# The first block of a graph-convolution kernel: its features loaded and cast in two halves, its slabs moved to the heads of two queues

## The chip, the cores and the metric

The kernel runs on one core of a Trainium2 chip. The metric is the device time of one execution in microseconds (us). The engines are named as in the profile: PE (TensorE matmul), PEld (its weight load), DVE (VectorE), ACT (ScalarE), POOL (GpSimd) and SP (SyncE, which here only issues loads).

## The reference, cut to what matters

Eight graphs share one sparse 2048 x 2048 adjacency matrix, whose nonzero values are equal within a row. Each of two layers multiplies the features by the matrix repeatedly, mixes the results with weights, adds the input and normalizes.

```
x: (8, 2048, 64)   adj: (2048, 2048), rows divided by their number of entries
# layer 0
A2  = 2 * (adj @ adj) - I
x_g = [x, adj x, A2 x]                        # per node
out = einsum('bnki,nkio->bno', x_g, w) + b    # w, b from the node's embedding
x   = layernorm(x + out)
# layer 1: five terms x, A x, (2 A A - I) x, and the last two again
x   = layernorm(x + concat(terms) @ weight + bias)
```

## The kernel before, in words

The nodes are cut into 16 tiles of 128. The adjacency matrix lies transposed in memory, so a slab `adj[h, k]` holds the 128 source nodes of tile k against one half h of the target nodes. A slab is not used as numbers: DVE turns it into zeros and ones (`places`, `tensor_scalar ... not_equal` with 0, written as float32r, into a tile `s`), and the row's common value, kept in `rcol`, is multiplied in when a sum leaves PSUM. The features of a tile (`z[0][k]`, 128 x 512) are split into a high part, a cast to float32r on ACT (`high`, line 250), and the remainder, a subtraction on DVE (`low`, line 254). Both parts are called `hl` and are the moving operand of the products.

The part of the kernel that matters here is the first hop, `hop_x(g, kk, j)`. It is run for g = 0, 1 (which quarter columns of the slabs are taken), kk = 0 to 7 and j = 0, 1, with k = kk + 8 j. So the first block works on tile 0 and the second on tile 8. One block is 16 products of 128 x 512: eight column groups i of the slab, each against the high and the low part (`add_block`, line 264). In the very first block the eight products with the high part come first, then the eight with the low part; from the second block on, the order is i by i, high then low. Group i = 0 to 3 of a g = 0 block reads `s[:, 0]` and i = 4 to 7 reads `s[:, 1]`.

`run` issues these steps in a hand-written order: the part `features` of a block four blocks ahead, `operands` two blocks ahead, `use` (the products) in its turn. Instructions wrapped in `ordered` or `load` stay in program order on their engine, so what is written later on DVE, ACT or SP waits for what is written earlier. In the first two blocks `features` loads two half slabs of 256 KB, `raws[0]` and `raws[1]`, each into its own one of the six `raw` buffers; later blocks load one tile of 512 KB.

Before all of this, `first_constants` loads the features of tile 0 (256 KB) and `rcol` (8 KB, 64 bytes for each partition) on the queue of ACT, while SP loads the slabs. It also loads ACT's function table and issues ten products on a tile of zeros (`WARM = 10`, line 145) so that TensorE is running before the first real product.

In the first block DVE runs `places` of the first half slab, then `low`, then `places` of the second half slab. In the second block it runs `low` and then both `places`:

```
high(z[0][k], hl)
if j == 1:
    low(z[0][k], hl)
for h in range(2):
    ordered(nc.vector.tensor_scalar(s[:, h], got["raws"][h], 0.0, None, ALU.not_equal))
    if h == 0 and j == 0:
        low(z[0][k], hl)
```

After the first hop come a second hop built on seven half-size products, the mixing of layer 0, and the same for layer 1 with a last stage that stores the output.

Of the kernel before, what the change touches and what calls it, by code (L numbers as in the profile page):

```python
# [9 lines left out]
F32 = mybir.dt.float32  # L10
# [4 lines left out]
ALU = mybir.AluOpType  # L15
# [3 lines left out]
P = 128  # L19
B, N, C = 8, 2048, 64  # L20
# [5 lines left out]
FIRST = 8  # L26
HL = 7
RAW = 6
WARM = 10
SLOTS = 3  # L30
SPLIT = 4096.0
SWAPPED = (0, 2, 1, 3, 4, 6, 5, 7)
# [9 lines left out]
def pattern(  # L42
# [22 lines left out]
    nc = tc.nc  # L65

    def pool(stack, name, bufs, **kw):
        return stack.enter_context(tc.tile_pool(name=name, bufs=bufs, **kw))
# [4 lines left out]
    rawp = pool(ctx, "fraw", RAW)  # L73
# [12 lines left out]
    def bank(name):  # L86

        return psum.tile([P, 2, 512], F32, tag="ps", name=name)
# [7 lines left out]
    z = [z0, [z1[:, t, :] for t in range(NT)], [z2[:, t, :] for t in range(NT)]]  # L96

    def bc(s, t):
        return z[s][t].rearrange("p (b c) -> p b c", c=C)


    rcol = keep.tile([P, NT], F32, tag="rcol", name="rcol")
# [21 lines left out]
    def load(q, to, src):  # L124
        return tc.keep_in_program_order(q.dma_start(out=to, in_=src))
# [3 lines left out]
    def ordered(ins):  # L129
        if in_order:  # L130
            tc.keep_in_program_order(ins)


    def first_constants():
        load(nc.scalar, z[0][0], x[0].rearrange("n b c -> n (b c)"))
        load(nc.scalar, rcol, rcols)
        nc.vector.memset(eps, EPS)

        tc.keep_in_program_order(nc.scalar.activation(root, eps, AF.Sqrt))

        idle = spool.tile([P, 5 * P], BF16, tag="s", name="idle")
        nc.vector.memset(idle, 0.0)
        first = bank("first")
        for _ in range(WARM):
            nc.tensor.matmul(first[:, 0, :], lhsT=idle[:, :P], rhs=idle[:, P:], start=True, stop=True)
        nc.vector.memset(part, 1.0 / C)
        nc.vector.memset(ident, 0.0)
        make_identity(nc, ident, nomemset=True)

    def node_bias(pb):  # L150

        eT, b0_sb = bias_sb, wl[:, 5]
        for j in range(4):
            for g in range(4):
                q = slice(32 * g, 32 * g + D)
                nc.tensor.matmul(  # L156
                    pb[g // 2][:, g % 2, j * C : (j + 1) * C], lhsT=eT[q, j * P : (j + 1) * P], rhs=b0_sb[q],
                    start=True, stop=True, tile_position=(32 * g, 0),
                )
# [67 lines left out]
    def load_slab(src, shape):  # L227
        raw = rawp.tile(shape, F32, tag="raw", name="raw")
        load(nc.sync, raw, src)
        return raw  # L230
# [6 lines left out]
    def places(raw):  # L237
        s = spool.tile(list(raw.shape), F32R, tag="s", name="s")
        ordered(nc.vector.tensor_scalar(s, raw, 0.0, None, ALU.not_equal))
        return s  # L240
# [8 lines left out]
    def high(src, to):  # L249
        ordered(nc.scalar.copy(to[0], src))  # L250

    def low(src, to):

        ordered(nc.vector.tensor_tensor(to[1], src, to[0], ALU.subtract))  # L254

    def halves(src, to=None):

        if to is None:
            to = [hpool.tile([P, B * C], F32R, tag="hl", name="hl") for _ in range(2)]
        high(src, to)  # L260
        low(src, to)
        return to

    def add_block(accs, s, hl, first, last):

        order = [(i, h) for i in range(len(accs)) for h in range(2)]
        if first:
            order.sort(key=lambda ih: ih[1])
        for i, h in order:
            nc.tensor.matmul(  # L270
                accs[i], lhsT=s[:, i * P : (i + 1) * P], rhs=hl[h],
                start=(first and h == 0), stop=(last and h == 1),
            )
# [19 lines left out]
    def banks(n):  # L293
        pairs = [bank("acc") for _ in range(n // 2)]
        return [p[:, i] for p in pairs for i in range(2)]
# [222 lines left out]
    Q = N // 4  # L518
    BC = B * C // 2
    KK = NT // 2  # L520
    first_constants()


    sums_of = scratch.tile([KK, 2, P, 4, Q], BF16, tag="sums", name="sums_of")
# [6 lines left out]
    def put_together(g, kk, x0, x1):  # L531
        to = z2[:, 2 * (kk % 8) : 2 * (kk % 8) + 2, :].rearrange("p t n -> p (t n)").bitcast(BF16)
        to = to.rearrange("p (i n) -> p i n", i=4)
        for i, (a, b, op) in enumerate((
            (x0[:, 1], x1[:, 1], ALU.add), (to[:, S1], x0[:, 0], ALU.subtract),
            (x1[:, 0], to[:, S2], ALU.subtract), (x0[:, 0], x0[:, 1], ALU.subtract),
        )):
            ordered(nc.vector.tensor_tensor(to[:, i], a, b, op))

        stores.append(lambda: ordered(nc.scalar.dma_start(out=sums_of[kk, g], in_=to)))  # L540

        for _ in range(2):
            if len(stores) > (1 if g else 6):
                stores.pop(0)()

    def hop_x(g, kk, j):
        k = kk + KK * j

        def features(got):
            if g == 0 and kk == 0:  # L550
                if j == 1:
                    load(nc.sync, z[0][k], x[k].rearrange("n b c -> n (b c)"))
                got["raws"] = [load_slab(adj[h, k, :, :Q], [P, Q]) for h in range(2)]

        def operands(got):
            if g == 0 and kk == 0:

                s = got["s"] = spool.tile([P, 2, Q], F32R, tag="s", name="s")
                hl = got["hl"] = [hpool.tile([P, B * C], F32R, tag="hl", name="hl") for _ in range(2)]
                high(z[0][k], hl)  # L560
                if j == 1:
                    low(z[0][k], hl)
                for h in range(2):
                    ordered(nc.vector.tensor_scalar(s[:, h], got["raws"][h], 0.0, None, ALU.not_equal))
                    if h == 0 and j == 0:
                        low(z[0][k], hl)
            else:
                if g == 0:
                    load(nc.sync, z[0][k], x[k].rearrange("n b c -> n (b c)"))
                raw = load_slab(adj[:, k, :, g * Q : (g + 1) * Q].rearrange("h m n -> m h n"), [P, 2, Q])  # L570
                got["s"] = places(raw)
                got["hl"] = halves(z[0][k])
                if g == 1 and len(loads) > 3:
                    load(nc.sync, *loads.pop(0))
            while due:
                due.pop(0)()
            couple.append(got["s"])
            if j == 1:
                due.append(lambda both=couple[:]: put_together(g, kk, *both))
                couple.clear()  # L580
                if g == 1 and kk == KK - 1:
                    due.pop(0)()

        def out(i):
            t = 4 * g + i if i < 4 else 4 * g + i + 4
            a, r = accs[i], rcol[:, t : t + 1]
            if i % 2 if g == 0 or i > 3 else i > 1:
                ordered(nc.vector.tensor_scalar_mul(z[1][t], a, r))
            else:
                ordered(nc.scalar.activation(z[1][t], a, AF.Copy, scale=r))  # L590

        def use(got):
            s, hl = got["s"], got["hl"]
            if kk == 0 and j == 0:
                accs[:] = banks(8)
            last = kk == KK - 1 and j == 1
            add_block(accs, s.rearrange("p h n -> p (h n)"), hl, kk == 0 and j == 0, last)
            if last:
                for i in range(8 if g == 0 else 4):
                    out(i)  # L600
            seen = xcpool.tile([P, 2, Q], BF16, tag="ln_xc", name="seen")
            i = g * NT + k
            ordered(nc.scalar.activation(seen, s, AF.Copy, accum_out=nonzero[:, i : i + 1]))
            if j == 1:
                ordered(nc.scalar.dma_start(out=quarters[kk, :, :, g, :], in_=seen))
            else:
                ordered(nc.scalar.dma_start(out=corner[kk, :, g, :], in_=seen[:, 0]))
            if k in centred and g == 1:
                centre_features(k)
            if last and g == 1:  # L610
                stores.pop(0)()

                todo.extend(lambda i=i: out(i) for i in range(4, 8))

        return [(4, features), (2, operands), (0, use)]


# [284 lines left out]
    s = ("load_sum", "operands")  # L902
    h, norm = None, None
# [3 lines left out]
    for t in range(NT):  # L907
        got, last = {}, t == NT - 1
# [62 lines left out]
        norm, h = norm_now, z[0][t]  # L971
# [487 lines left out]
```

## Time and profile before

| | |
|---|---|
| median of 4 runs | 751.27 us (750.83, 750.84, 751.69, 751.72) |
| the profiled execution | 750.95 us, of which the span from the first to the last instruction is 748.6 us |
| granted TensorE clock, mean | 0.997 |
| PE busy | 740.4 us, 99% of the span |
| DVE, ACT, POOL busy | 80%, 61%, 39% |
| first warming product, first real product | 1.29 us, 5.13 us |
| products of the first hop, lines L270 and `acc` | 512 in 116.61 us |

A share of busy time is an average over the whole span. What the first few microseconds contain is read from the timeline and from windows of half a microsecond. In the timeline, the columns are the start, the length, the engine, the line, the operation with what it writes and reads, the shape, the number of instructions that were merged into the line, and in brackets how long the engine had been idle and what ended that.

### The profile page before, as it was taken

The page shows a single profiled execution, that of the slowest core. Times are in us where ns is not written, and L with a number is a line of the kernel's source. Part 1 is how long each engine was busy: PE and PEld are TensorE (multiplying, and loading weights), DVE is VectorE, ACT ScalarE, POOL GpSimd, SP SyncE. Part 2 cuts the span into 40 slices and gives each one's busy share as a digit, 9 for nine tenths or more (in the row PEclk, how much of TensorE's full clock was granted, in tenths as well). Part 3 has the DMA queues.
Part 4 walks back from the last instruction along what each step waited for, and adds up shares of the span by engine and source line. Part 5 has one row for each costly group of instructions (what it writes and reads, how often), then busy time and mean ns, then how long its engine had stood idle before and what let it go on. Part 6 is the DMA issues. An engine that isn't in the chain of part 4 may idle for free.

```text
span 748.6 us, 13524 instructions
## 1 busy us (share of the span) xinstructions
PE 740.4 (99%) x4940; PEld 613.3 (82%) x4940; DVE 598.7 (80%) x954; ACT 456.7 (61%) x1123; POOL 293.2 (39%) x312
## 2 busy tenths in 40 slices
PE   9999999999999999999999999999999999999996
PEld 6888888888888888888888888888888888888885
DVE  6868888999978898888888888869588557778663
ACT  5445453878766677777777777778877662112111
POOL 0001110133233888888888888874000000021431
PEclk9999999999999999999999999999999999999998
DMA  8996997545420000000000000003444354665621
GB/s 313 354 381 214 377 385 258 179 158 165 159 86 15 17 15 16 18 17 26 6 25 15 16 15 1 2 29 128 136 159 146 136 168 142 176 184 176 197 99 46
DMA packets 73544, 96.47 MB, mean 129 GB/s; under 512 B 4864, under 2 KB 48384, under 8 KB 73344
## 3 DMA queue, kind: packets, MB, share of 16 engines
q1 hardware_dynamic: 62064, 76.66, 31.6%
q10 hardware_dynamic: 11408, 18.89, 6.8%
q8 instruction: 41, 0.67, 0.4%
q14 instruction: 31, 0.25, 0.1%
HBM read 76.65 MB, written 18.87 MB: 128 GB/s over the span
## 4 chain that ended last, share of the span: by engine, by line
PE 98%; DMA 0%; DVE 0%; ACT 0%; issue 0%; DVEq 0%; ACTq 0%
PE pm L426 35%; PE accT L707 27%; PE acc L270 16%; PE a L270 10%; PE accT L270 6%; PE pu L501 3%; PE pt L316 1%; PE accT L863 1%; DMA z<-in_x 0%; PE accT L501 0%; PE accT L156 0%; PE accT L316 0%; ACT hl L250 0%; DVE z L305 0%; DVE sq L1078 0%
## 5 line engine op out<-in xcount | busy, mean ns | idle before, releaser
L707 PE MATMUL accT<-s,hl 128*128 128x512 f32 x896 | 205.8, 391 | 0.0
L707 PEld LDWEIGHTS accT<-s,hl 128*128 128x128 f32 x896 | 167.5, 188 | 35.5 <-issue 0.5
L460 ACT ACTIVATE aside<-pm,pack_sb 128x128 f32<-128x128 f32 x512 | 141.8, 436 | 18.9 <-PE pm L426 16.3
L426 PE MATMUL pm<-wh,hl 64*128 64x512 f32 x768 | 151.6, 392 | 0.0
L426 PE MATMUL pm<-wm,parts 64*128 64x512 f32 x768 | 149.8, 387 | 0.0
L426 PE MATMUL pm<-wl,parts 64*128 64x512 f32 x768 | 149.6, 386 | 0.0
L694 ACT CAST s<-raw 128x1024 fp32r<-128x1024 bf16 x104 | 110.1, 1058 | 36.8 <-ACT hl L250 27.9
L270 PE MATMUL acc<-hl,s 128*128 128x512 f32 x512 | 116.6, 390 | 0.2 <-ACT hl L250 0.2
L476 DVE TENSOR_REDUCE sums<-aside 128x128 f32<-128x1024 f32 x96 | 112.6, 1213 | 1.4
L270 PEld LDWEIGHTS acc<-hl,s 128*128 128x128 f32 x512 | 95.9, 188 | 21.0 <-ACT hl L250 0.7
L447 DVE TENSOR_TENSOR aside<-pm,pack_sb 128x1024 f32<-128x1024 f32 x64 | 78.0, 1222 | 18.5 <-PE pm L426 18.1
L426 PEld LDWEIGHTS pm<-wm,parts 64*128 64x128 f32 x768 | 72.0, 184 | 15.3
L426 PEld LDWEIGHTS pm<-wh,hl 64*128 64x128 f32 x768 | 72.2, 185 | 14.7 <-issue 0.4
L426 PEld LDWEIGHTS pm<-wl,parts 64*128 64x128 f32 x768 | 72.1, 184 | 14.4
L250 ACT CAST hl<-z 128x256 fp32r<-128x256 f32 (+1 forms) x96 | 47.8, 516 | 58.4 <-PE acc L270 24.2
L406 POOL TENSOR_TENSOR s<-s,part 128x8 f32<-128x8 f32 x16 | 7.0, 440 | 172.8 <-DVE s L405 102.7
L270 PE MATMUL a<-hl,s 128*128 128x512 f32 (+1 forms) x352 | 73.4, 370 | 0.0
L254 DVE TENSOR_TENSOR hl<-z,hl 128x512 fp32r<-128x512 f32 (+1 forms) x96 | 58.0, 611 | 18.2 <-ACT hl L250 8.0
L465 POOL TENSOR_TENSOR aside<-aside 128x1024 f32<-128x1024 f32 (+2 forms) x48 | 70.9, 1477 | 2.5
L270 PEld LDWEIGHTS a<-hl,s 128*128 128x128 f32 x352 | 61.9, 188 | 11.3
L303 POOL TENSOR_TENSOR z<-z,got 128x512 f32<-128x512 f32 x3 | 4.8, 1624 | 143.4 <-ACT got L302 143.4
L371 ACT ACTIVATE sq<-z 128x512 f32<-128x512 f32 x31 | 20.0, 652 | 48.2 <-DVE z L305 46.9
(139 smaller groups left out, 955.2 us busy)
## 6 DMA issues: line engine op xcount, KB each, us to landing
raw<-in_adj SPq DMA_DIRECT2D x58, 512.0 KB, 6.0
raw<-sums_of SPq DMA_DIRECT2D x64, 256.0 KB, 2.7
sums_of<-z ACTq DMA_DIRECT2D x16, 512.0 KB, 7.4
raw<-quarters SPq DMA_DIRECT2D x32, 256.0 KB, 2.6
raw<-in_adj SPq DMA_DIRECT2D x16, 384.0 KB, 3.5
quarters<-seen ACTq DMA_DIRECT2D x16, 256.0 KB, 6.6
xt<-in_xT SPq DMA_DIRECT2D x16, 256.0 KB, 2.7
z<-in_x SPq DMA_DIRECT2D x15, 256.0 KB, 6.1
```

The costliest lines, as they stand in the source:

```text
L250: ordered(nc.scalar.copy(to[0], src))
L254: ordered(nc.vector.tensor_tensor(to[1], src, to[0], ALU.subtract))
L270: nc.tensor.matmul(accs[i], lhsT=s[:, i * P : (i + 1) * P], rhs=hl[h], start=(first and h == 0), stop=(last and h == 1),)
L371: ordered(nc.scalar.activation(sq, src, AF.Square))
L426: nc.tensor.matmul(pm[:, j], lhsT=tt[k][n][q, u, :], rhs=w_parts[n][k][q, ds, :], start=(k == 0 and n == 0), stop=(k == 2 and n == 2),)
L447: ordered(nc.vector.tensor_tensor(side_by_side(a), got, e, ALU.mult))
L460: ordered(nc.scalar.activation(to[d], got, AF.Copy, scale=emb_sb[:, t, h * DD + d : h * DD + d + 1]))
L465: ordered(nc.gpsimd.tensor_tensor(to, to, more, ALU.add))
L476: ordered(nc.vector.tensor_reduce(to, src, AX.X, ALU.add))
L501: nc.tensor.matmul(pm[:, j, i * 3 * C : (i + 1) * 3 * C], lhsT=hT[q, 2 * g + i, :], rhs=v[q], start=True, stop=True,)
L694: ordered(nc.scalar.copy(s, got["raw"]))
L707: nc.tensor.matmul(acc[i][:, c], lhsT=hl[h][:, i * P : (i + 1) * P], rhs=S[:, c * 512 : (c + 1) * 512], start=(kk == 0 and h == 0), stop=( ...
```

## The change

The features of tile 0 are loaded in two halves of 128 KB (the graphs 0 to 3 and 4 to 7): the first at the head of ACT's queue, the second on SP's queue behind the first half slab. The second half slab goes from SP's queue to ACT's, behind the first half of the features. The cast of tile 0 is divided: ACT casts the first half, DVE (`tensor_copy`) the second. `places` of the first half slab is cut into 128 and 384 columns, and the order on DVE in the first block becomes copy, `places` of 128, of 384 and of 512 columns, then `low`. The second block loads its slab as one transfer of 512 KB instead of two of 256 KB, and its order on DVE becomes `places`, `places`, `low`. `rcol` is loaded on SP's queue with the third pair of blocks. Seven warming products are issued instead of ten.

```diff
-WARM = 10
+WARM = 7
...
     def first_constants():
-        load(nc.scalar, z[0][0], x[0].rearrange("n b c -> n (b c)"))
-        load(nc.scalar, rcol, rcols)
+        raws = [rawp.tile([P, N // 4], F32, tag="raw", name="raw") for _ in range(2)]
+        halves_of_x = slice(0, B // 2), slice(B // 2, B)
+        load(nc.sync, raws[0], adj[0, 0, :, : N // 4])
+        for q, b in zip((nc.scalar, nc.sync), halves_of_x):
+            load(q, bc(0, 0)[:, b], x[0][:, b])
+        load(nc.scalar, raws[1], adj[1, 0, :, : N // 4])
...
+        return raws
...
-    first_constants()
+    first_raws = first_constants()
...
                 if j == 1:
                     load(nc.sync, z[0][k], x[k].rearrange("n b c -> n (b c)"))
-                got["raws"] = [load_slab(adj[h, k, :, :Q], [P, Q]) for h in range(2)]
+                    got["raw"] = load_slab(adj[:, k, :, :Q].rearrange("h m n -> m h n"), [P, 2, Q])
...
-                high(z[0][k], hl)
+
+                def place(to, raw):
+                    ordered(nc.vector.tensor_scalar(to, raw, 0.0, None, ALU.not_equal))
+
                 if j == 1:
-                    low(z[0][k], hl)
-                for h in range(2):
-                    ordered(nc.vector.tensor_scalar(s[:, h], got["raws"][h], 0.0, None, ALU.not_equal))
-                    if h == 0 and j == 0:
-                        low(z[0][k], hl)
+                    high(z[0][k], hl)
+                    for h in range(2):
+                        place(s[:, h], got["raw"][:, h])
+                else:
+                    ordered(nc.vector.tensor_copy(hl[0][:, BC:], z[0][k][:, BC:]))
+                    ordered(nc.scalar.copy(hl[0][:, :BC], z[0][k][:, :BC]))
+                    for h, c in ((0, slice(0, P)), (0, slice(P, Q)), (1, slice(0, Q))):
+                        place(s[:, h, c], first_raws[h][:, c])
+                low(z[0][k], hl)
             else:
                 if g == 0:
                     load(nc.sync, z[0][k], x[k].rearrange("n b c -> n (b c)"))
+                    if kk == 2 and j == 0:
+                        load(nc.sync, rcol, rcols)
```

## The prediction

> **What bounds the kernel now.** I read the chain of waits first, in order of time.
>
> ```profile
> 0.74 3.70 DMA z<-in_x
> 4.46 0.63 ACT hl L250
> 5.08 0.04 issue
> 5.13 116.61 PE acc L270 x512
> ```
>
> From 5.13 us the chain runs through PE alone until the last products end at 741.94 us. Before it stand one load, one cast and a semaphore. So the change can act in two places only: in the 5.13 us ahead of the first product, and in stalls between early products. The same view has 398 products of the same size (accT, L707) in 90.44 us, 0.227 us each. At that pace 512 take 116.3 us, so the first hop loses 0.3 us. The timelines of DVE and PEld show where, and what the second block waits for.
>
> ```profile
> 4.28 0.43 DVE L564 TENSOR_SCALAR s<-raw 128x512 fp32r<-128x512 f32 x1 [2.90 <-DMA raw<-in_adj]
> 5.11 0.69 DVE L254 TENSOR_TENSOR hl<-z,hl 128x512 fp32r<-128x512 f32 x1 [0.40 <-ACT hl L250]
> 5.72 0.42 DVE L564 TENSOR_SCALAR s<-raw 128x512 fp32r<-128x512 f32 x1
> 6.95 0.69 DVE L254 TENSOR_TENSOR hl<-z,hl 128x512 fp32r<-128x512 f32 x1 [0.81 <-ACT hl L250]
> 7.56 0.42 DVE L564 TENSOR_SCALAR s<-raw 128x512 fp32r<-128x512 f32 x1
> 8.15 0.43 DVE L564 TENSOR_SCALAR s<-raw 128x512 fp32r<-128x512 f32 x1 [0.18 <-DMA raw<-in_adj]
> 10.18 0.69 DVE L239 TENSOR_SCALAR s<-raw 128x1024 fp32r<-128x1024 f32 x1 [1.60 <-DMA raw<-in_adj]
> ```
>
> ```profile
> 5.13 0.77 PEld L270 LDWEIGHTS acc<-hl,s 128*128 128x128 f32 x4 [0.70 <-ACT hl L250]
> 6.19 3.06 PEld L270 LDWEIGHTS acc<-hl,s 128*128 128x128 f32 x14 [0.30 <-DVE s L564]
> ```
>
> The fifth weight load waits for the second half slab's `places` (5.72 + 0.42 = 6.14). Each of the two starts costs about 0.1 us of refilling. The 17th product, the first of block 2, thus starts near 5.13 + 16 x 0.227 + 0.3 = 9.06, and the 18th, the first with block 2's low part, at 9.29. That low part is ready at 6.95 + 0.69 = 7.64 and block 2's last `places` at 8.58: block 2 waits for nothing, with 0.5 us in hand.
>
> The DMA engines, last (columns: busy time of five engines, clock, DMA share, GB/s):
>
> ```profile
> 2.50:3.00 0.50, 0.50 (x3) 0.18 (x2) 0.00 (x0) 0.49 (x2) 0.00 (x0) 1.00 0.50 164
> 3.00:3.50 0.50, 0.50 (x3) 0.22 (x2) 0.00 (x0) 0.16 (x1) 0.00 (x0) 1.00 1.05 410
> 4.50:5.00 0.50, 0.42 (x2) 0.00 (x0) 0.21 (x1) 0.50 (x1) 0.00 (x0) 1.00 0.83 259
> 6.50:7.00 0.50, 0.50 (x4) 0.38 (x3) 0.05 (x1) 0.42 (x1) 0.00 (x0) 1.00 1.05 393
> ```
>
> From 3 us on they are full, except near 4.5 to 5.0, when `rcol` with its 128 pieces of 64 bytes is in flight. A load here is worth its bytes at about 390 GB/s and its place in the order.
>
> **The first block, step by step.** Four loads hold the same 768 KB as features, slab and slab held before; only the order differs. The first half of the features shares the engines with the first half slab, as the whole features did, and being half as large it lands no later than 4.44. The second half is behind the slab on SP's queue, beside the second half slab on ACT's. Before, 512 KB had to move until the features were there (4.44). Now at least the same 512 KB has to, and at most all 768 KB: 256 KB at 360 GB/s is 0.73 us, so it lands between 4.4 and 5.17. SP's queue was the faster at the beginning (slab in by 4.28, features by 4.46, issued together), so ACT's second half slab is still mostly waiting then; I take 4.6, near the early end.
>
> DVE starts 0.02 after a landing, and an operation begins 0.08 before the end of the one ahead (5.11 + 0.69 against 5.72). `places` costs 0.424 for 512 columns and 0.689 for 1024 (rows of L564 and L239), so 0.16 + 0.52 per 1000: 0.225 for 128 and 0.36 for 384. DVE's cast of 256 columns has no row; as a `tensor_scalar` it would be 0.29, as DVE's subtraction of 256 columns (L639) 0.45. I take 0.29: like `places`, it has one input. ACT's cast of its half is 0.412 (row of L250, 128x256) and ends by 4.9, beside this. DVE holds its three `places` and `low` in order behind the copy, so a slab that is ready at 4.28 now waits for features:
> - copy from 4.62 to 4.91, 128 columns to 5.06, 384 columns to 5.34. First product at 5.06 + 0.04 = 5.10, against 5.13.
> - The second product needs the 384 columns: weights from 5.38, 0.19 for a load (mean of PEld L270), so 5.57. Before, it came at 5.47 (two products from 5.13 end at 5.87, each 0.39).
> - The second half slab lands by 5.2 to 5.6, its `places` ends by 6.0, and the fifth product wants it at 6.2: that stall goes. `low` ends near 6.6 and is wanted at 7.1.
>
> So the 18th product would start at 5.57 + 16 x 0.227 = 9.20 instead of 9.29: 0.09 gained. Halving a cast of 0.62 buys that little, since the half on DVE pushes two `places` (0.15 + 0.28) onto the path.
>
> **The second block.** This order adds a wait. `low` was done before the slab came; now it is queued on DVE behind both `places`, and both wait for one 512 KB load. From that load's landing T: 0.02, two `places` at 0.34 from start to start, `low` 0.69, 0.04 and a weight load 0.19 to 0.20, in all T + 1.63. PE's second product of the block waits for it and all behind it. Bounds for T: 8.13, where the last half slab lands now with the same bytes ahead, and 7.6, which is the features of tile 8 (in at 6.27) plus 512 KB at 390 GB/s. Without `rcol` ahead (131 GB/s missing for 0.5 us, or 0.17 us) I take 8.0, since the present landing is the nearer row. The 18th product starts at 9.63, which is 0.34 later than now; the first block's gain is swallowed. Only T below 7.57 avoids this.
>
> **The rest at nothing, with its cover.** `rcol` on SP costs one issue (0.4) and 0.2 us of the DMA engines ahead of the third pair's slab; that block's `places` now starts at 14.05 and its products near 20, and `rcol` is first read after the 16 blocks of g = 0, some 58 us later. Without that cover it would cost 0.2. One `raw` buffer becomes free, so a later slab can be issued earlier, but the DMA engines are full. Three warming products fewer end the warming near 4.1 to 4.3 instead of 4.9; PE waits until 5.10 for data in either case. ACT's second issue replaces one of the same length (0.45). The table load behind it ends at 2.95 and hides.
>
> **Sum.** 750.95 (span 748.6 and 2.35 around it) + 0.34 = 751.29. The median of the runs shown is 0.32 above the profiled one, in two pairs near 750.84 and 751.70; the forecast for a median is 751.27 + 0.34 = 751.6.
>
> [...]
>
> **Rivals.**
> 1. *The opening wins.* Second half in at 4.4, double load by 7.35. First product 4.90, 18th at 9.00 against T + 1.63 = 8.98. Gain 0.29: 751.0. For it: no `rcol` in the way. Against: the 8.13 of today. Chance 0.18.
> 2. *The halves come late*, at 5.17, since both queues share evenly. First product 5.67, 18th at 9.77, later than the `low` path. Loss 0.48: 751.75. Chance 0.20.
> 3. *The clock is lost (the slower side).* Weight loads of the warming products start 0.43 apart up to 3.82, and the last three within 0.6: the array doubles its pace after some 2.6 us of work, although the clock column shows 1.00. With seven, PE idles 0.8 to 1.0 us before the first product, where it idled 0.21. If that sends it back to the slow pace for 2.6 us, six products take 0.43 instead of 0.227: 1.2 less the 0.09 gained is +1.1, 752.4. From a slow spell of 3.4 us on it passes 1.5 us. Against it: PE has worked for 2.8 of the 3.8 us before. Chance 0.08; half of it beyond 1.5 us.
> 4. *The double load is later than all rows*, T over 9.2, because ACT's slab takes engines from SP's: 1 us for each us, over +1.5. Chance 0.03.
>
> [...]
>
> **Chances and range.** Forecast 0.51, rivals 0.18, 0.20, 0.08, 0.03. A measurement of this kernel can tell about 0.2%, 1.5 us. No case gains that much, for the first product can't come before the slab's 4.28: faster 0.02. Slower: half of rival 3, rival 4 and an unknown 0.01: 0.07. Within: 0.91. The range takes rival 1 and 2 with the two pairs of runs (0.4 either way around the median): 750.8 to 752.4.
>
> **What would show it.** Right: a first real product at 4.9 to 5.3, no wait before the fifth, and a wait of PEld for DVE's `hl` (L254) near 9, with idle time of 0.2 to 0.6. Wrong: no such wait, a first product after 5.6 with ACT and DVE waiting for `z<-in_x`, or weight loads 0.43 apart after the start.

## The result, and the profile after

The changed kernel is slower by 0.14%: its median over 32 executions is 752.63 us, that of the kernel before over 52 executions is 751.29 us, and the ratio is 1.0014 with a 95% interval of 1.0009 to 1.0019, or 1.05 us. The forecast was no change that can be told, with 0.3 us more as the likeliest. The ratio applied to the 751.27 us known before gives 752.3, inside the range of 750.8 to 752.4; the bare median of 752.63 is 0.2 above its upper end.

The 32 times do not lie around one value. Eight are between 751.0 and 751.45, as fast as the kernel before; nineteen are above 752.3, where none of these 52 executions of before is (of those that ran beside the experiments below, one is, at 752.34). Something happens in some executions and not in others. The profiled execution, 752.59 us with a span of 750.6, is one of the slower ones. First its chain of waits, in order of time (start, length, what):

```profile
0.73 0.39 SPq L125
1.13 0.06 issue
1.19 3.84 DMA z<-in_x
5.05 0.29 DVE hl L574
5.34 0.15 DVE s L567
5.49 0.14 issue
5.63 117.90 PE acc L275 x512
```

Two things changed. The chain now runs through SP's second load, the second half of the features, which lands at 5.03; with the copy, the short `places` and the way to PE, the first product starts at 5.63 instead of 5.13. And the 512 products of the first hop take 117.90 us instead of 116.61. The rest keeps its length: the last products end at 743.77 instead of 741.94, and 0.50 + 1.29 of these 1.83 us are in the two lines above.

The 1.29 us are in the first eight products. The timeline of DVE, PEld and PE:

```profile
5.05 0.29 DVE L574 CAST hl<-z 128x256 fp32r<-128x256 f32 x1 [3.67 <-DMA z<-in_x]
5.26 0.82 DVE L567 TENSOR_SCALAR s<-raw 128x128 fp32r<-128x128 f32 x3
5.60 10.47 PEld L275 LDWEIGHTS acc<-hl,s 128*128 128x128 f32 x40 [2.05 <-ACT hl L575]
5.63 10.64 PE L275 MATMUL acc<-hl,s 128*128 128x512 f32 x39 [1.18 <-DVE s L567]
8.19 0.77 DVE L567 TENSOR_SCALAR s<-raw 128x512 fp32r<-128x512 f32 x2 [1.51 <-DMA raw<-in_adj]
8.87 0.69 DVE L259 TENSOR_TENSOR hl<-z,hl 128x512 fp32r<-128x512 f32 x1
```

The 39 products take 0.273 us each on average where 0.227 is full pace (398 products of the same size, L721, in 90.44 us of this profile), and no wait stands between them. The windows show which ones are slow. From the kernel before, and then from the changed one (us from:to, length, busy time and instructions of PE, PEld, DVE, ACT, POOL, then clock, DMA share, GB/s):

```profile
6.00:8.00 2.00, 2.00 (x10) 1.51 (x9) 1.17 (x3) 0.62 (x1) 0.00 (x0) 1.00 1.00 367
```

```profile
6.00:8.00 2.00, 2.00 (x6) 1.52 (x6) 0.69 (x2) 0.56 (x1) 0.00 (x0) 1.00 1.03 302
8.00:10.00 2.00, 2.00 (x9) 1.58 (x8) 1.37 (x3) 1.12 (x2) 0.00 (x0) 1.00 1.04 385
```

PE is busy in all of them, but in the first two microseconds it works on six products instead of ten. The count in parentheses (products that run in the window at all), not the busy share, tells the pace; the clock column stays at 1.00 in all three lines and does not show it. The trace's list of clock changes explains the column: it has no entry before full clock is first granted, and a stretch without an entry is shown as 1.00. That first entry stands at 3.96 us in the profile of before and at 8.84 us in this one. Until then the products of the high part run some 0.427 us apart, like the warming products, and the eight cost 8 x 0.2 = 1.6 us, less the 0.3 of stalls that the kernel before had there. TensorE was at half pace not again, but still:

```profile
1.28 3.17 PE L149 MATMUL first<-idle 128*128 128x512 bf16 x7 [1.28 <-DVE idle L146]
5.63 7.69 PE L275 MATMUL acc<-hl,s 128*128 128x512 f32 x26 [1.18 <-DVE s L567]
```

The seven warming products end at 4.45 without having sped up, and PE then idles for 1.18 us.

The wait that the forecast rested on is not in this profile. The low part of block 2 (8.87 + 0.69 = 9.56) is ready long before the 18th product, which starts at 11.12. The quicker executions of this kernel have no profile; with full pace from 5.63 on they would want the low part at about 9.5, an estimate from 17 steps of 0.227.

### The profile page after: what moved, and what is told of

It reads as the page before. It is cut to its first block, busy times and chain, and to the rows that moved or that the text cites. A ratio compares the mean times of both kernels' runs of the same rounds, so it can differ in the third digit from the quotient of the medians.

```text
span 750.6 us, 13515 instructions
## 1 busy us (share of the span) xinstructions
PE 741.3 (99%) x4937; PEld 613.8 (82%) x4937; DVE 598.3 (80%) x956; ACT 456.9 (61%) x1123; POOL 292.2 (39%) x312
## 4 chain that ended last, share of the span: by engine, by line
PE 98%; DMA 1%; DVE 0%; issue 0%; SPq 0%; ACT 0%; DVEq 0%; ACTq 0%
PE pm L431 35%; PE accT L721 27%; PE acc L275 16%; PE a L275 10%; PE accT L275 6%; PE pu L506 3%; PE pt L321 1%; PE accT L877 1%; DMA z<-in_x 1%; PE accT L506 0%; PE accT L161 0%; PE accT L321 0%; DVE z L310 0%; SPq L125 0%; DVE sq L1092 0%
## 5 line engine op out<-in xcount | busy, mean ns | idle before, releaser
L721 PE MATMUL accT<-s,hl 128*128 128x512 f32 x896 | 205.8, 390 | 0.0
L721 PEld LDWEIGHTS accT<-s,hl 128*128 128x128 f32 x896 | 167.5, 188 | 35.6 <-issue 0.5
L255 ACT CAST hl<-z 128x512 fp32r<-128x512 f32 (+1 forms) x95 | 47.2, 515 | 59.0 <-PE acc L275 31.0
```

The lines of the kernel that those rows point to most:

```text
L721: nc.tensor.matmul(acc[i][:, c], lhsT=hl[h][:, i * P : (i + 1) * P], rhs=S[:, c * 512 : (c + 1) * 512], start=(kk == 0 and h == 0), stop=( ...
```

## The experiments

Each ratio below is against executions of the kernel before that ran beside the kernel in question, so it can differ from the ratio of two medians in this text.

**How much warming.** Two theories were tried first. By the clock theory the loss is half pace. By the data theory it is the late second half of the features. The number of warming products was set back alone, raised, and lowered in the kernel before, where the loads are the old ones.

```diff
-WARM = 7
+WARM = 10
```

> The changed kernel with ten warming products again, nothing else. Clock theory (too little warming work ahead of a longer idle gap leaves TensorE at half pace for the first eight real products, 0.427 instead of 0.227 us each, 1.6 us): the products start near 5.63 as in the changed kernel but at 0.227 us each in most executions, and the median falls by 1.0 to 1.4 us, to 751.2 to 751.6, with no executions near 753. Data theory (the loss is the second half of the features landing at 5.03, not the clock): the median stays at 752.3 to 752.7. The wait that I predicted for the second block's low part shows here, if it exists: about 0.2 us before the 18th product, because it is no longer hidden by half pace.

Measured: 751.33 us, 0.9997 of the kernel before (0.9989 to 1.0006), and none of 11 executions above 752.3. The loss is gone with three instructions.

```profile
6.00:8.00 2.00, 2.00 (x8) 1.64 (x9) 1.03 (x3) 0.62 (x1) 0.00 (x0) 1.00 0.94 326
8.00:10.00 2.00, 2.00 (x11) 1.64 (x10) 1.32 (x4) 1.43 (x2) 0.00 (x0) 1.00 1.05 397
```

Full clock comes at 6.47 us in that profile. Its second half of the features landed even later, at 5.25, and its first product came later, at 5.85:

```profile
5.28 0.29 DVE L574 CAST hl<-z 128x256 fp32r<-128x256 f32 x1 [3.89 <-DMA z<-in_x]
```

```profile
1.29 4.45 PE L149 MATMUL first<-idle 128*128 128x512 bf16 x10 [1.29 <-DVE idle L146]
5.85 7.38 PE L275 MATMUL acc<-hl,s 128*128 128x512 f32 x30
```

So the data theory is out as the cause of the loss. What the later first product costs by itself is not visible in these times: the interval ends at 0.45 us above the kernel before. The predicted wait before the 18th product did not appear here either, which my expectation had at 0.2 us: that product starts at 10.12, and the low part is ready at 9.24. A cost of 0.34 us lies inside the interval, so this rests on the profile alone.

The same edit in the kernel before, downward:

```diff
-WARM = 10
+WARM = 7     # and, in a second kernel, 4
```

> The kernel before with seven warming products instead of ten, nothing else: the idle gap before its first real product at 5.13 grows from 0.2 to about 0.9 us. Clock theory: part of its executions start at half pace, so the times spread out upward to 753 and the median rises by 0.2 to 1.2 us, to 751.5 to 752.5. Data theory: no difference, 751.3, since the loads and casts are those of before.

> The kernel before with four warming products, nothing else: they end near 3.0 and leave 2.1 us of idle time before the first product at 5.2. [...]

Measured with seven: 7 of 12 executions from 750.50 to 751.42, 5 from 752.49 to 753.70; median 751.34, ratio 1.0003 (0.9995 to 1.0012). The median alone would say that nothing happened, and misses the expected rise; the spread is what was expected. Measured with four: 10 of 11 above 752.3, median 753.29, ratio 1.0024 (1.0015 to 1.0033). The profiled execution with four:

```profile
1.29 1.89 PE L145 MATMUL first<-idle 128*128 128x512 bf16 x4 [1.29 <-DVE idle L142]
5.36 8.02 PE L270 MATMUL acc<-hl,s 128*128 128x512 f32 x23 [2.19 <-ACT hl L250]
```

```profile
6.00:8.00 2.00, 2.00 (x6) 1.60 (x5) 0.87 (x3) 0.62 (x1) 0.00 (x0) 1.00 1.02 386
8.00:10.00 2.00, 2.00 (x6) 1.52 (x5) 0.87 (x3) 1.13 (x2) 0.00 (x0) 1.00 1.03 386
```

Half pace holds through both windows, so up to 10 us; full clock comes at 10.74, and in the profile with seven, one of the five slow executions (753.12), at 9.57. In all profiles of this document with nine to thirteen warming products it comes between 3.96 and 7.22. So seven and four warming products with the old loads make the same slow start, and by the times above 752.3 (5 of 12 and 10 of 11), the more often the fewer they are.

```diff
-WARM = 7
+WARM = 13
```

> The changed kernel with thirteen warming products, which fill the time up to about 5.56, just short of its first real product at 5.63. Clock theory, if the idle gap itself matters: 0 to 0.3 us below the run with ten, and a narrower spread. If only the amount of warming work by 4 to 5 us matters: equal to the run with ten within 0.2 us. Data theory: equal to the changed kernel, 752.6.

Measured: 751.87 us, 1.0005 (0.9996 to 1.0014), and 4 of 11 executions above 752.3, but none above 752.61. So it is not better than ten, against the expectation; whether it is worse, the two intervals don't tell. A possible reason is that thirteen products at half pace last until 1.29 + 13 x 0.427 = 6.84 and then hold back the first real product themselves. The profiled execution had full pace before they ended (from 4.75 on) and so doesn't show it; this remains an inference.

**What delays the second half.** The half slab on ACT's queue was put behind the features on SP's queue.

```diff
-        load(nc.scalar, raws[1], adj[1, 0, :, : N // 4])
+        load(nc.sync, raws[1], adj[1, 0, :, : N // 4])     # and WARM = 10
```

> The changed kernel with ten warming products and with the second half slab on SP's queue behind the second half of the features, so that only 512 KB compete until the features are complete. If that slab on ACT's queue is what delays the second half (5.03 in the changed kernel): it lands at 4.4 to 4.6, the first product comes at 4.9 to 5.2, and the median is 0.1 to 0.5 us below the run with ten alone. If SP's queue order alone sets it (features behind a slab): it still lands at 5.0 and the time is equal to the run with ten.

Measured: the second half lands at 4.64 and the first product comes at 5.24, as expected. With the slab on ACT's queue the half landed at 4.86, 5.03 and 5.25 (thirteen, seven and ten warming products); in this kernel and its two edits below it landed at 4.64, 4.70 and 4.78. So the slab on ACT's queue is what delays it, by 0.1 to 0.6 us. But the time is 752.84, 1.0021 of before (1.0012 to 1.0029), against the expected gain. DVE, PE and PEld of that run:

```profile
4.66 0.29 DVE L574 CAST hl<-z 128x256 fp32r<-128x256 f32 x1 [3.27 <-DMA z<-in_x]
9.61 0.76 DVE L567 TENSOR_SCALAR s<-raw 128x512 fp32r<-128x512 f32 x2 [3.25 <-DMA raw<-in_adj]
10.18 0.47 PE L275 MATMUL acc<-hl,s 128*128 128x512 f32 x1 [1.03 <-DVE s L567]
11.02 0.99 PEld L275 LDWEIGHTS acc<-hl,s 128*128 128x128 f32 x5 [0.69 <-DVE hl L259]
11.03 2.33 PE L275 MATMUL acc<-hl,s 128*128 128x512 f32 x9 [0.37 <-DVE hl L259]
```

Block 2's slab lands at 9.59; in the run with ten it was 7.86. PE runs dry, first for the `places` (17th product, 10.18), then for the low part queued behind them (18th, 11.03): this is the predicted wait, with the fourth rival's late load, in another kernel, and not for that rival's reason, since here no slab is on ACT's queue. The windows show where the time went:

```profile
5.00:5.50 0.50, 0.50 (x3) 0.27 (x2) 0.50 (x3) 0.00 (x0) 0.00 (x0) 1.00 1.18 291
5.50:6.00 0.50, 0.50 (x3) 0.43 (x3) 0.50 (x2) 0.00 (x0) 0.00 (x0) 1.00 0.67 98
6.00:6.50 0.50, 0.50 (x4) 0.40 (x3) 0.36 (x1) 0.00 (x0) 0.00 (x0) 1.00 0.66 156
```

For a microsecond the loads move 98 to 156 GB/s, where they moved 336 to 391 between 3 and 5 us. Five edits looked for the cause of this and of the wait.

```diff
-                    got["raw"] = load_slab(adj[:, k, :, :Q].rearrange("h m n -> m h n"), [P, 2, Q])
+                    got["raws"] = [load_slab(adj[h, k, :, :Q], [P, Q]) for h in range(2)]
```

> The kernel with ten warming products and the second half slab on SP's queue, in which the second block's slab landed at 9.6 and the first product came at 5.24, now with that slab as two loads of 256 KB again. If the single load of 512 KB is what makes it late: both halves are in by 8.2, the block starts near 9.0 and the median falls from 752.84 to 750.9 to 751.5. If the order of the queue does it (SP now has all loads but one in a row): the last half still lands after 9, and the median stays above 752.3.

Measured: 752.70 us, 1.0016 (1.0007 to 1.0025). The slow stretch stays (201 and 197 GB/s from 6.0 to 7.0), and the last half lands at 9.31. The size of the load is not the cause.

```diff
                     high(z[0][k], hl)
+                    low(z[0][k], hl)
                     for h in range(2):
                         place(s[:, h], got["raw"][:, h])
```

> The same kernel (ten warming products, second half slab on SP's queue, one load of 512 KB) with one step moved: in the second block the low part is computed ahead of both places, as in the kernel before. My prediction's step says that the low part behind the places costs what it keeps the 18th product waiting: in the run without this edit the 17th product starts at 10.18 and the 18th at 11.03, 0.6 more than the spacing of 0.23. So here the 18th follows the 17th by 0.23 to 0.34, and the median falls by 0.4 to 0.7 us, to 752.1 to 752.4. A rival (the places, not the low part, are what the block waits for) gives no change, 752.8. The slab's landing at 9.6 should stay.

Measured: 752.24 us, 1.0012 (1.0003 to 1.0021). The slab still lands late, at 9.62, but there is one start instead of two:

```profile
10.19 1.92 PEld L275 LDWEIGHTS acc<-hl,s 128*128 128x128 f32 x9 [0.47 <-issue]
```

The 18th product now follows the 17th by 0.31 us instead of 0.85. So the low part behind the places costs 0.5 us in the profile where the slab is that late. In the times, the ratio falls from 1.0021 to 1.0012, but the two intervals overlap: consistent with it, not proof. In the kernel before, the same step costs nothing:

```diff
                 high(z[0][k], hl)
-                if j == 1:
-                    low(z[0][k], hl)
                 for h in range(2):
...
+                if j == 1:
+                    low(z[0][k], hl)
```

> The kernel before with one step moved: in the second block the low part is computed behind both places instead of ahead of them. My prediction priced this step at 0.34 us with the changed kernel's loads. Here the last half slab lands near 8.1, its places begin there, the low part ends at about 9.2, and the 18th product wants it at 9.29: so 0 to 0.1 us where the first product comes at 5.13 or later, and the median is within 0.2 us of the kernel before. If the low part behind the places is what made the changed kernel slower, the median rises by 0.3 to 1.0 us.

Measured: 751.45 us, 1.0000 (0.9991 to 1.0009). So the order costs nothing that can be told here. Its profile has the slab in at 8.46, the low part ready at 9.52 and the 18th product at 9.95, but full clock came only at 6.68 there; with an early clock that product would come at some 9.4 (estimated from 5.21, 17 steps of 0.227 and the 0.3 of stalls seen before), and no profile shows that case.

> Ten warming products, the low part first in the second block, all slabs on SP's queue, and both halves of the features on ACT's queue, so that SP's queue holds slabs only until the features of tile 8. Two things stay open: why the loads slow down to between 98 and 300 GB/s at 5 to 7.5 us in every kernel that has a half of the features on SP's queue. If that half on SP's queue is the cause: 340 to 406 GB/s from 3 us on as in the kernel before, the second block's slab in by 8.2, first product at 4.8 to 5.1, no waits, and a median 0.1 to 0.5 us below the kernel before run beside it. If it has another cause: the slow stretch stays, the slab lands after 9, and the time is 0.5 to 1.3 us above it.

The edit to the kernel with the low part first is `zip((nc.scalar, nc.scalar), halves_of_x)`. Measured: 751.92 us, 1.0003 (0.9994 to 1.0013). The deep stretch is gone (the lowest window is 270 GB/s) and the slab is in at 7.78, as expected if the half on SP's queue has to do with it. But the second half of the features now lands at 5.55, the latest of all, against the 4.4 to 4.6 that my numbers need. By 5.36 SP's queue had both its slabs in, 512 KB, while ACT's needed until 5.55 for 256 KB. The two queues from 3 to 5 us (SP's is q1, ACT's q10; packets, MB, share of the engines' time):

```profile
q1 hardware_dynamic: 285, 0.52, 67.8%
q10 hardware_dynamic: 254, 0.23, 34.2%
```

Nearly as many packets went through one queue as through the other, 254 and 285, but with 0.9 KB on average against 1.8: in the traces of the kernel before and of the changed one a packet of the halves holds 1 KB (half a row of the features) and one of the slabs 2 KB, with some of 4 bytes on both queues. So in these two microseconds ACT's queue, with the halves, moved at about half the rate of SP's, 0.23 MB against 0.52.

This profile also shows that the idle time alone is not what costs:

```profile
1.29 3.67 PE L149 MATMUL first<-idle 128*128 128x512 bf16 x10 [1.29 <-DVE idle L146]
6.15 7.08 PE L275 MATMUL acc<-hl,s 128*128 128x512 f32 x30 [1.19 <-DVE s L567]
```

PE idles for 1.19 us, as long as in the changed kernel, but full clock had been granted at 4.05, during the ten warming products, and the real products run at full pace from the start. None of the 11 executions is above 752.3. So here the gap did not take full clock away; after seven products it had not yet been granted (8.84 in the changed kernel, 9.57 in the kernel before with seven).

> The kernel before with only rcol moved to SP's queue with the third pair of blocks. My prediction priced this at nothing, with 0.17 us of transfer time gained ahead of the second block's slab. If so: the same median within 0.2 us, full rate from 3 us on and the last half slab in near 8.0. If the small transfer on ACT's queue was what kept the loads of SP's queue from slowing down at 5 to 7.5 us: the slow stretch appears here too, the last half slab lands near 9, and the median rises by up to 0.7 us.

The edit is the last hunk of the change, in the kernel before. Measured: 751.35 us, 1.0001 (0.9992 to 1.0010). The move of `rcol` costs nothing. But a milder slow stretch is here too:

```profile
6.50:7.00 0.50, 0.50 (x3) 0.38 (x3) 0.29 (x2) 0.20 (x1) 0.00 (x0) 1.00 1.00 287
7.00:7.50 0.50, 0.50 (x4) 0.41 (x3) 0.50 (x2) 0.00 (x0) 0.00 (x0) 1.00 0.98 283
```

So the mild form, 270 to 300 GB/s, needs none of the halves. Nor does it need the move of `rcol`: the kernel before with seven warming products has 287 GB/s from 6.0 to 6.5, and the one with the low part last 295 from 7.0 to 7.5, both with the loads of before. The deep form, half a microsecond or more below 205 GB/s after the first 3 us, appeared in the profiles of the four kernels with a half of the features and all first slabs on SP's queue (the one shown, the first two edits of it, and the next below) and in no other. The reason is open.

**Versions meant to beat both.** The first takes what must move before the first product down to 320 KB. The diff shows its loads; it also has ten warming products, two loads for the second block and the low part first. The second keeps all loads of before, divides the cast and the first `places`, and has nine warming products.

```diff
-        load(nc.sync, raws[0], adj[0, 0, :, : N // 4])
+        load(nc.sync, raws[0][:, :P], adj[0, 0, :, :P])
         for q, b in zip((nc.scalar, nc.sync), halves_of_x):
             load(q, bc(0, 0)[:, b], x[0][:, b])
-        load(nc.scalar, raws[1], adj[1, 0, :, : N // 4])
+        load(nc.sync, raws[0][:, P:], adj[0, 0, :, P : N // 4])
+        load(nc.sync, raws[1], adj[1, 0, :, : N // 4])
```

> A version made to keep the early start and drop the costs: ten warming products, the features in halves at the heads of both queues, the first half slab cut into 128 and 384 columns around the second half of the features, all slabs on SP's queue, two loads and the low part first for the second block. Only 320 KB have to move until the first product can start. If bytes in the order of need set the start: second half in at 4.1 to 4.4, first product at 4.6 to 4.9, and with no wait in the second block a median of 750.6 to 751.2, 0.4 to 0.9 us below the kernel before run beside it. If TensorE's clock rises at a time of its own, an earlier start is worth only half of what it seems, 0.2 to 0.4 us, which lies at the edge of what can be measured.

Measured: 751.91 us, 1.0008 (0.9999 to 1.0017). The second half lands at 3.62, a microsecond earlier than in any other kernel, and the first product starts at 4.86. Then the same stretch comes earlier, and the second product waits for the 384 columns:

```profile
3.50:4.00 0.50, 0.50 (x3) 0.20 (x2) 0.36 (x2) 0.23 (x1) 0.00 (x0) 1.00 0.44 105
```

```profile
4.86 0.58 PE L276 MATMUL acc<-hl,s 128*128 128x512 f32 x1
6.22 7.09 PE L276 MATMUL acc<-hl,s 128*128 128x512 f32 x30 [0.78 <-DVE s L568]
```

> The loads, queues and second block of the kernel before, with only the division of the first cast between ACT and DVE, the places of the first half slab in 128 and 384 columns, and nine warming products. The cast's two halves run side by side from about 4.46, so the first product comes at 4.9 to 5.0 instead of 5.13 where the warming products are done by then; nine of them at half pace end at 5.13, ten at 5.55. If the cast of 0.62 us is worth shortening: 0.1 to 0.4 us below the kernel before. If the loads and the clock set the start, no difference that can be measured.

Measured: 751.24 us, 0.9996 (0.9987 to 1.0005). Its first product comes at 5.05 with the features landing at 4.57. No version beats the kernel before by more than the measurement tells.

## Why the prediction was right and wrong

The sign and the size class held: slower, by less than 0.2%. The path to it did not. That the ratio lies in the range is luck: the loss came from the third rival, with its chance of 0.08, and not from the wait behind the forecast. The prediction's own signs of being wrong all came: no such wait, a first product after 5.6, and products 0.43 us apart after the start.

- *The second half's landing.* The step took 4.6 from the bounds 4.4 to 5.17, since SP's queue was ahead at the beginning (slab in by 4.28, features by 4.46). It landed at 5.03, and at 4.86 and 5.25 in the kernels with other warming. That is near the second rival's condition (5.17), and the first product came at 5.63, near its 5.67. The run with the slab on SP's queue shows that this slab was the cause (4.64 there). The first half, though half as large, came only 0.07 us earlier than the whole had (4.37 against 4.44), which would fit its packets of half the size (1 KB against 2 KB); no run tests that. The steps after the landing were right in their kinds and 0.1 us short: 0.29 for the copy and 0.23 for 128 columns as taken, but 0.14 us, not 0.04, from `places` to the product.
- *The second block's wait.* This was the forecast's 0.34 us, and in the changed kernel's profile it does not occur. The products reach block 2 later than assumed (the 18th comes at 11.12, where the prediction had it wanted at 9.20). The same order in the kernel before measured 1.0000 (0.9991 to 1.0009, which does not exclude 0.34 us). Where the wait does occur, the 18th product starts 1.44 us after the slab lands (9.59 to 11.03), not 1.63: its weight load starts at 11.02 and the product at 11.03, so the 0.19 of the load do not stand between the low part and the product.
- *The clock.* The third rival had a chance of 0.08. That PE is at half pace after seven products and a gap of 1.18 us holds in the profile (0.427 us from product to product until 8.84), by the times in some 19 of 32 executions, and gives the whole loss that can be told: with ten products the ratio is 0.9997. But the rival had the gap send PE back to half pace, and that is not what happened: the clock had not risen at all, and after ten products, with full clock from 4.05, a gap of 1.19 us did no harm. The premise behind it, that the array speeds up after 2.6 us of work, was read from one profile; with ten products the rise came anywhere from 3.96 to 7.22 us, so 2.7 to 5.9 us after the first. I argued against the rival that PE had worked for 2.8 of the 3.8 us before. With the landing 0.4 later, the gap was wider than the 0.8 to 1.0 assumed. But seven products are too few even with the loads of before (5 of 12), so the chance was too small by itself. Its price, 1.2 us for six products, was near: eight products cost 1.6, less the 0.3 of stalls that vanish.
- *At nothing.* `rcol` on SP's queue was rightly priced (1.0001). The three warming products were not: they were costed by what waits for PE, and not by what they do to the products after them.

What sets the moment of the rise, and how much work ahead of it is enough in every execution, no run here measures. The profiles show only that it moves: it stands at 3.96, 6.47 and 8.84 us in those of before, of the run with ten and of the changed kernel, and the changed kernel's times split into two groups from execution to execution.

## What to carry to other kernels

In this kernel the warming work had to be enough for the clock to rise in nearly every execution before the real products came, or soon after. By the executions above 752.3 us, ten products were (none of 11 in the changed kernel with ten, and none of 11 where a gap of 1.19 us follows them); seven and four, with the loads of before, were not (5 of 12 and 10 of 11). If an edit moves the first product or shortens the warming, judge by the spread of many executions, not by one or by the median: the rise itself moved by 3 us, from 3.96 to 7.22, between profiles with the same ten products. Read the pace of TensorE from products per window or from their spacing, since neither the busy share (2.00 of 2.00 us) nor the clock column (1.00) shows half pace here, where six products run in 2 us instead of ten. When a load is moved to a second queue so that two things land together, ask what shares the engines with the later one, and how large the packets of each are: the first half of the features landed on time and the second, on which everything waited, did not.

## What the runs showed that I had not expected

Where the second half of the features and all first slabs were on SP's queue, the features came in earlier (at 4.64 to 4.78 and 3.62 instead of 4.86 to 5.25), and for a microsecond or more around or after their landing the DMA engines moved only 98 to 201 GB/s: at 5.5 to 7 us where they landed at 4.64 to 4.78, with 324 to 391 GB/s between 3 and 5 us before it, and at 3 to 4.5 us where they landed at 3.62. Thirteen warming products were no better than ten, which, at half pace, already reach to 5.56 us (an estimate, 1.29 + 10 x 0.427).
